# Projecting attention heads with fixed weights, and sending the inverse sums through DRAM: layer 3 of a four-layer graph network

## The chip, the core and the metric

The kernel runs on one core of one Trainium2 chip. The time is the device time of one execution in microseconds (us). The core has a matrix engine (PE) with its weight loads (PEld), a vector engine (DVE), a scalar engine (ACT), a general engine (POOL), and a sync engine (SP) that here issues nearly all DMAs. Each engine works through its own queue in order and waits on semaphores of the others.

## The reference

Sixteen graphs ("batches") of 1024 nodes with 64 features go through four layers over one adjacency matrix, each followed by a residual and a normalisation. The change is in layer 3 only, which computes, per batch:

```python
h = jnp.einsum('bnc,hdc->bhnd', x, Wh)             # 4 heads of 64 channels
out_h = _gat_layer(h, mask, bh)                    # softmax(h h^T, masked) h + bias, per head
cat = jnp.transpose(out_h, (0, 2, 1, 3)).reshape(B, N, H * D)
z = leaky_relu(cat, 0.2)
h2 = jnp.einsum('bnk,dk->bnd', z, Wo)              # 256 channels to 64
out2 = _gat_layer(h2, mask, bo)                    # the outer attention, one head
z2 = leaky_relu(out2, 0.2)                         # then a layer norm with gamma, beta
```

Afterwards the residual with x and one more normalisation give the output of the batch.

## The kernel before

Layer 3 takes a little over two thirds of the time. Its heads are worked in two pairs, n = 0 and n = 1. A pair's attention is 16 **units** (8 blocks of 128 nodes by 2 halves h of 512 nodes). A unit has four steps: `scores` on PE (L1336, two 64-row matmuls into a PSUM tile `s` from a ring of three buffers), an exponential on ACT (L1340, with a constant `shift` per batch and pair that keeps it in range, into a tile `e` from a ring of 11), a mask product on DVE (L1344), and `product` on PE (L1351), which adds the unit to the unnormalised output `y` with channels on partitions and nodes along the row. One value column is all ones, so one channel of each head (rows 63 and 127 of the pair) holds the softmax sum. The outer attention has 8 units of the same kind (L1438, L1443, a sum on DVE at L1448, the mask at L1456, L1463).

The units of a batch are dealt into eight **bursts**, written out by hand: bursts 0 to 3 have five units of the heads, bursts 4 to 7 three of the heads and two outer units of the batch before. `run` puts a burst j into the queues in this order: pending small steps (`catch_up`), the scores and exponentials of the burst, tasks hung on the burst as **mids**, the products of the burst before (`drain`), the masks of this burst, tasks hung on it as **slots**. Engines keep that order.

```python
            catch_up()
            made = [(unit, unit[0]()) for unit in burst]
            tasks(mids, b, j)
            while roots:
                roots.pop(0)()
            drain()
            made = [(product, mask(e)) for (_, mask, product), e in made]
            waiting.extend(lambda product=product, e=e: product(e) for product, e in made)
            ...
            tasks(slots, b, j)
```

From the heads to the outer attention a batch has a **chain** of tasks, each with a place (burst, counted from the start of its batch, so that 8 is burst 0 of the next one):

- `project(q)`, four times (pair by half; 3, 5, 7, 9 mids). The half of `y` was copied to the tile `yT` by ACT (L1357). PE multiplies each 128-node block of it, as the stationary operand, with the weights `wb` (L1366), which gives nodes on partitions and, in two extra columns, the sums. DVE copies the sums (L1370), takes reciprocals (L1372), multiplies (L1376) and applies the leaky relu (L786) into `z`.
- `z_T(n)`, twice (8 mids, 9 slots): eight transposes on PE (L1399) and an ACT copy (L1400) turn a pair's `z` back to channels on partitions, `zT`.
- `h_2T` (10 mids): PE multiplies `zT` with `woT` (L1411), first for n = 0, then n = 1; ACT copies the result to `h2T` (L1415) and squares it; DVE copies two halves across (L1417, L1418).
- `shift_of` (11 mids): PE sums the squares (`pn`, L1273), DVE takes the maximum `top` (L1277), POOL spreads it over partitions (`gtop`, L1279), and the step `below` on ACT turns it into `shift` (L1284). `below` waits in the list `soon`, which `catch_up` puts at the start of the next burst.
- `h_2v` (12 mids): transposes of `h2T`. The first outer units are in burst 12.

After the outer units the ends of a batch follow: `gather` (18 mids: transposes `po2` on PE, L1493, and the product v, L1507, on DVE), `layer` (bias bo and leaky, 18 slots), mean and centre (L726 to L732, 19 slots), and further normalising steps up to the store of `res` by SP. The last two batches and the one before have places of their own. The same functions also prepare the head projections of the next two batches (`prep_x`, `prep_h` with further calls of `shift_of`).

Of the kernel before, what the change touches and what calls it, by code (L numbers as in the profile page):

```python
# [8 lines left out]
F32 = mybir.dt.float32  # L9
# [4 lines left out]
ALU = mybir.AluOpType  # L14
AX = mybir.AxisListType

P = 128
# [565 lines left out]
def fast_path(  # L583
# [24 lines left out]
    nc = tc.nc  # L608
    B, N, D = x.shape
    C = N // P  # L610
    H = L3_Wh.shape[0]
    HD = H * D
    NP = HD // P
    GB = 4
    NG = B // GB
    HALF = N // 2
    CH = C // 2
# [3 lines left out]
    small = ctx.enter_context(tc.tile_pool(name="small", bufs=4))  # L621
# [23 lines left out]
    ident = const.tile([P, P], F32, tag="ident", name="ident")  # L645
# [139 lines left out]
    def leaky(dst, v):  # L785
        nc.vector.scalar_tensor_tensor(dst, v, ALPHA, v, ALU.mult, ALU.max)  # L786
# [407 lines left out]
    woT = const.tile([P, NP, D], F32, tag="woT", name="woT")  # L1194
    wb = const.tile([P, NP, P + 2], F32, tag="wb", name="wb")
    pair_ones = const.tile([P, 2], BF16, tag="pair_ones", name="pair_ones")
    sums = const.tile([P, B, H + 1, C], F32, tag="sums", name="sums")
# [55 lines left out]
    def nodes_adj(c):  # L1253
# [9 lines left out]
            nc.vector.tensor_tensor(own, own, ident16, ALU.max)  # L1263

        return convert
    xT2, hTs, shifts, vals, zs = {}, {}, {}, {}, {}

    def shift_of(key, sq):

# [57 lines left out]
    def heads(b, n):  # L1327
        held = {}

        def scores(k, h):  # L1330
            s = ps_s.tile([P, 2, HALF], F32, tag="s", name="s")
            hT = hTs[b, n][0]
            cols = slice(h * HALF, (h + 1) * HALF)
            for i in range(2):
                rows = slice(i * D, (i + 1) * D)
                nc.tensor.matmul(  # L1336
                    s[:, i, :], hT[rows, k * P : (k + 1) * P], hT[rows, cols], start=True, stop=True
                )
            e = l3.tile([P, 2, HALF], F32, tag="e", name="e", bufs=11)
            nc.scalar.activation(e, s, AF.Exp, bias=shifts[b, n])  # L1340
            return e

        def mask(k, h, e):
            nc.vector.tensor_tensor(e, e, bc_mid(aT[:, k, h * HALF : (h + 1) * HALF], 2), ALU.mult)  # L1344
            return e

        def product(k, h, e):
            if k == 0:
                held[h] = ps_h.tile([P, HALF], F32, tag=f"acc{h * (1 - n)}", name=f"y_{b}_{n}_{h}")
            for i in range(2):  # L1350
                nc.tensor.matmul(  # L1351
                    held[h][i * D : (i + 1) * D, :], vals[b][:, k, :], e[:, i, :],
                    start=(k == 0), stop=(k == C - 1),
                )
            if k == C - 1:
                held["y"] = l3.tile([P, HALF], F32, tag="y", name=f"yT_{b}_{n}_{h}", bufs=1)
                nc.scalar.copy(held["y"], held[h])  # L1357

        def project(q):

            if n == 0 and q == 0:
                zs[b] = l3.tile([P, C, HD], F32, tag="z", name=f"z_{b}", bufs=1)
            pt = ps_s.tile([P, 2, HALF], F32, tag="s", name="po")
            o = pt[:, :, : 2 * (P + 2)].rearrange("p t (c f) -> p t c f", c=2)
            for j in range(CH):
                nc.tensor.matmul(  # L1366
                    o[:, j // 2, j % 2, :], held["y"][:, j * P : (j + 1) * P], wb[:, n, :], start=True, stop=True,
                )
            total = sums[:, b, 2 * n : 2 * n + 2, q * CH : (q + 1) * CH]
            nc.vector.tensor_copy(total.rearrange("p i (t c) -> p t c i", t=2), o[:, :, :, P : P + 2])  # L1370
            rt = small.tile([P, 2, CH], F32, tag="rt3", name="rt3")
            nc.vector.reciprocal(rt, total)  # L1372
            v = l3.tile([P, CH, P], F32, tag="v3", name="v3", bufs=1)
            for i in range(2):
                cols = slice(i * D, (i + 1) * D)
                nc.vector.tensor_tensor(  # L1376
                    v[:, :, cols].rearrange("p (t c) d -> p t c d", t=2), o[:, :, :, cols],
                    rt[:, i].rearrange("p (t c) -> p t c", t=2).unsqueeze(3).to_broadcast([P, 2, 2, D]), ALU.mult,
                )
            leaky(zs[b][:, q * CH : (q + 1) * CH, n * P : (n + 1) * P], v)  # L1380

        units = [
            (lambda k=k, h=h: scores(k, h), lambda e, k=k, h=h: mask(k, h, e), lambda e, k=k, h=h: product(k, h, e))
            for h in range(2) for k in range(C)
        ]
        return units, project


    BURSTS, LAST = 8, 5

    def prep_out(b):
        st = {}

        def z_T(n):
            if n == 0:
                st["zT"] = l3.tile([P, NP, N], F32, tag="zT", name=f"zT_{b}", bufs=1)
            pt = ps_s.tile([P, C, P], F32, tag="s", name="pzT")
            for c in range(C):
                nc.tensor.transpose(pt[:, c, :], zs[b][:, c, n * P : (n + 1) * P], ident)  # L1399
            nc.scalar.copy(st["zT"][:, n, :], pt.rearrange("p c q -> p (c q)"))  # L1400

        def h_2T():


            hT = l3.tile([P, 2, HALF], F32, tag="h2T", name=f"h2T_{b}", bufs=1)
            sq = l3.tile([P, HALF], BF16, tag="h2sq", name=f"h2sq_{b}", bufs=1)
            hTs[b] = hT, sq
            pt = one_bank("ph2T")
            for n in range(NP):
                for h in range(2):  # L1410
                    nc.tensor.matmul(  # L1411
                        pt[h * D : (h + 1) * D, :], woT[:, n], st["zT"][:, n, h * HALF : (h + 1) * HALF],
                        start=(n == 0), stop=(n == NP - 1),
                    )
            nc.scalar.copy(hT[:, 0, :], pt)  # L1415
            nc.scalar.activation(sq, hT[:, 0, :], AF.Square)
            nc.vector.tensor_copy(hT[:D, 1, :], hT[D:, 0, :])  # L1417
            nc.vector.tensor_copy(hT[D:, 1, :], hT[:D, 0, :])  # L1418

        def h_2v():  # L1420
            v = l3.tile([P, C, D], F32, tag="h2v", name=f"h2v_{b}", bufs=1)
            pt = one_bank("ph2v").rearrange("p (c d) -> p c d", c=C)
            for c in range(C):
                nc.tensor.transpose(pt[:, c, :], hTs[b][0][:D, c // CH, c % CH * P : (c % CH + 1) * P], ident[:D, :D])
            nc.scalar.copy(v, pt)
            vals["out", b] = v

        return z_T, h_2T, h_2v
# [245 lines left out]
    with tc.tile_pool(name="ps_g", bufs=1, space=bass.MemoryType.PSUM, reuse_waits="tile") as ps_g, tc.tile_pool(  # L1674
        name="ps_u", bufs=2, space=bass.MemoryType.PSUM, reuse_waits="tile"
# [34 lines left out]
        for q, todo in enumerate(l1_tasks):  # L1710
            t = 7 + 2 * q
            places = (t, 0), (t, 2), (t, 4), (t, 6), (t + 2, 2), (t + 2, 7), (t + 3, 5)
# [13 lines left out]
    with tc.tile_pool(name="l1", bufs=2, reuse_waits="tile") as pool:  # L1726
# [36 lines left out]
        for g in range(NG):  # L1763
# [8 lines left out]
            st = pool.tile([P, C * GB, 6], F32, tag="st1", name=f"st{g}")  # L1772
# [5 lines left out]
            y = xg[g].rearrange("p c b d -> p (c b) d")  # L1778
# [21 lines left out]
    slots, mids = {}, {}  # L1800
    work = [[heads(b, n) for n in range(NP)] for b in range(B)]
    outs = [(prep_out(b), head_out(b)) for b in range(B)]
    E = B - 1
# [7 lines left out]
        at((c + 1) // BURSTS, (c + 1) % BURSTS, lambda convert=convert: convert["go"]())  # L1811
    for b in range(B):
        z_T, h_2T, h_2v = outs[b][0]
        parts = [lambda p=work[b][n][1], q=q: p(q) for n in range(NP) for q in range(2)]
        chain = [
            *parts[:2], lambda z_T=z_T: z_T(0), *parts[2:], lambda z_T=z_T: z_T(1), h_2T,
            lambda b=b: shift_of(b, hTs[b][1]), h_2v,
        ]
        ends = outs[b][1][1]

        places = [(3, mids), (5, mids), (8, mids), (7, mids), (9, mids), (9, slots), (10, mids), (11, mids), (12, mids)]
        places += [(18, mids), *((j, slots) for j in (18, 19, 19, 20, 22, 24, 24, 24, 25, 28))]
        if b == E - 2:
            places[9:] = [(17, mids), *((j, slots) for j in (17, 17, 18, 18, 20, 20, 21, 22, 22, 24))]
        elif b == E - 1:
            places[9:] = [(j, slots) for j in (15, 15, 15, 15, 15, 17, 17, 17, 18, 18)]
        elif b == E:
            places[2] = 7, mids
            places[4:] = [(j, slots) for j in [7] * 5 + [10] * 11]
        for task, (j, where) in zip(chain + ends, places):  # L1830
            t = min(j // BURSTS, E - b)
            at(b + t, j - t * BURSTS, task, where)
# [33 lines left out]
    with tc.tile_pool(name="ps_g", bufs=1, space=bass.MemoryType.PSUM, reuse_waits="tile") as ps_g, tc.tile_pool(  # L1866
        name="ps_p", bufs=1, space=bass.MemoryType.PSUM, reuse_waits="tile"
    ) as ps_p:
        places = [(15, j) for j in (0, 1, 2, 3, 4, 5, 6, 7)]
# [16 lines left out]
    l3 = ctx.enter_context(tc.tile_pool(name="l3", bufs=2, reuse_waits="tile"))  # L1886
    ps_h = ctx.enter_context(tc.tile_pool(name="ps_h", bufs=1, space=bass.MemoryType.PSUM, reuse_waits="tile"))
    ps_s = ctx.enter_context(tc.tile_pool(name="ps_s", bufs=3, space=bass.MemoryType.PSUM, reuse_waits="tile"))
    rings["s"] = ps_s
    aN = l3.tile([P, C, N], BF16, tag="aN", name="aN", bufs=1)  # L1890

    def tasks(where, b, j):
        for task in where.get((b, j), []):
# [110 lines left out]
```

## Time and profile before

| What | Before |
|---|---|
| Median of 3 runs | 2073.36 us (2067.45 to 2074.19) |
| Span of the profiled execution | 2072.9 us |
| PE busy | 1963.8 us |
| DVE busy | 1795.8 us |
| ACT busy | 1293.9 us |
| POOL busy | 70.1 us |
| Granted PE clock, mean | 0.982 |

The profiled execution's own time is its span of 2072.9 us, 0.5 us below the median of the runs. A row of the costliest groups gives line, engine, operation, output and inputs with shapes, count, then busy us and mean ns, then the idle time before it and what ended it. A row of the timeline gives start and length in us, then the same names, with the idle time of that engine before it in brackets. A row of busy times gives a stretch, its length, then the busy us of PE, PEld, DVE, ACT and POOL (with instruction counts), the granted clock, and the DMA share and rate. A row of DMA issues gives count, size of one, and the median us to landing. PE, f32 matmuls show as two instructions each. Line numbers are those of the kernel before unless said otherwise; the changed file is longer by up to 35 lines from this place on.

### The profile page before, as it was taken

What the parts mean: (1) busy time and instruction counts of PE and PEld (TensorE: products, weight loads), DVE (VectorE), ACT (ScalarE), POOL (GpSimd) and SP (SyncE); (2) the same over time, 40 slices, a digit from 0 to 9 for tenths busy, and PEclk for the clock granted to TensorE, in tenths of its full rate; (3) what the DMA queues carried; (4) which work ended last, traced back from release to release, by engine and by line L of the source; (5) the groups of instructions that cost most, each with busy time, mean ns of one, the idle gap of its engine ahead of it and who ended that gap; (6) DMA issues with size and microseconds to landing.
All of it is one profiled execution on the core that took longest, in us unless ns stands there. A gap on an engine that the chain in (4) does not pass through costs nothing.

```text
span 2072.9 us, 26628 instructions
## 1 busy us (share of the span) xinstructions
PE 1963.8 (95%) x10041; PEld 854.1 (41%) x10041; DVE 1795.8 (87%) x3147; ACT 1293.9 (62%) x2250; POOL 70.1 (3%) x77
## 2 busy tenths in 40 slices
PE   7999989998898999999999999999999999999985
PEld 4444347753332343343343434434343343433432
DVE  5899988879998777889898898988989889889996
ACT  4466568676778666666666656656665665665543
POOL 0000000000000000000000000000000000000001
PEclk9999999999999999999999999999999999999997
DMA  7000000000000200000000000000000000000000
GB/s 170 1 1 1 1 1 1 1 1 1 1 1 11 71 1 1 1 1 6 1 6 6 1 6 6 1 6 1 6 1 6 6 1 6 6 1 6 1 6 17
DMA packets 23657, 18.92 MB, mean 9 GB/s; under 512 B 19361, under 2 KB 19426, under 8 KB 23522
## 3 DMA queue, kind: packets, MB, share of 16 engines
q1 hardware_dynamic: 23218, 17.11, 3.0%
q8 instruction: 81, 1.33, 0.3%
q14 instruction: 54, 0.44, 0.1%
q10 hardware_dynamic: 304, 0.03, 0.0%
HBM read 12.95 MB, written 4.19 MB: 8 GB/s over the span
## 4 chain that ended last, share of the span: by engine, by line
PE 47%; DVE 37%; ACT 11%; issue 3%; DMA 0%; POOL 0%; SPq 0%; DVEq 0%; POOLq 0%; ACTq 0%
DVE e L1344 13%; PE y L1351 10%; PE s L1336 8%; DVE e L991 6%; PE y_l L1003 6%; ACT e L1340 6%; PE po L1735 5%; DVE e L1456 4%; DVE junk L1448 4%; PE u_l L1015 3%; PE y L1463 2%; PE po L1366 2%; ACT e L1443 2%; PE s L1438 2%; DVE v L1376 2%
## 5 line engine op out<-in xcount | busy, mean ns | idle before, releaser
L1340 ACT ACTIVATE e<-s,shift 128x1024 f32<-128x1024 f32 x512 | 542.8, 1119 | 335.3 <-PE s L1336 334.3
L1344 DVE TENSOR_TENSOR e<-e,aT 128x1024 f32<-128x1024 f32 x512 | 600.7, 1217 | 4.9 <-ACT e L1340 4.8
L1351 PE MATMUL y<-e,vals 128*64 128x512 f32 x2048 | 489.5, 600 | 11.0 <-DVE e L1344 5.9
L1336 PE MATMUL s<-hT 64*128 64x512 f32 x2048 | 497.8, 605 | 1.3 <-ACT e L1340 0.9
L991 DVE SCALAR_TENSOR_TENSOR e<-G_l,q,aT 128x1024 f32<-128x1024 f32 x256 | 315.3, 1274 | 4.4 <-ACT G_l L968 4.4
L1336 PEld LDWEIGHTS s<-hT 64*128 64x128 f32 x2048 | 186.9, 187 | 279.7 <-issue 141.1
L1003 PE MATMUL y_l<-e,vals_l 128*64 128x512 f32 x1024 | 257.7, 624 | 25.4 <-DVE e L991 18.7
L1351 PEld LDWEIGHTS y<-e,vals 128*64 128x64 f32 x2048 | 134.9, 136 | 277.8 <-issue 189.6
L1456 DVE TENSOR_TENSOR e<-e,aT 128x1024 f32<-128x1024 f32 x128 | 156.3, 1224 | 8.3 <-ACT e L1443 1.9
L1448 DVE SCALAR_TENSOR_TENSOR junk<-e,aN 128x1024 bf16<-128x1024 f32 x120 | 146.1, 1218 | 0.0
L1443 ACT ACTIVATE e<-s,shift 128x1024 f32<-128x1024 f32 x128 | 142.0, 1115 | 1.3 <-PE s L1438 1.1
L1463 PE MATMUL y<-e,h2v 128*64 128x512 f32 x512 | 131.2, 595 | 1.5 <-DVE e L1456 1.5
L1438 PE MATMUL s<-h2T 64*128 64x512 f32 x512 | 131.7, 596 | 0.0
L1003 PEld LDWEIGHTS y_l<-e,vals_l 128*64 128x64 f32 x1024 | 63.6, 140 | 160.8 <-issue 78.4
L1735 PE MATMUL po<-hi,aR 128*128 128x512 f32 x256 | 104.1, 407 | 11.1 <-ACT hi L1664 7.3
L1735 PE MATMUL po<-lo,aR 128*128 128x512 f32 x256 | 102.3, 400 | 0.0
L1279 POOL PARTITION_ALL_REDUCE gtop<-top x48 | 42.7, 890 | 1375.9 <-DVE top L1277 1236.4
L780 ACT ACTIVATE x<-m,bn_shift,bn_rstd 128x64 f32<-128x64 f32 x256 | 88.5, 431 | 0.5 <-DVE bn_shift L771 0.5
L1366 PE MATMUL po<-wb,yT 128*128 128x130 f32 x512 | 74.2, 288 | 10.1 <-ACT e L1340 9.4
L1366 PEld LDWEIGHTS po<-wb,yT 128*128 128x128 f32 x512 | 61.9, 190 | 47.4 <-ACT e L1340 45.8
L1438 PEld LDWEIGHTS s<-h2T 64*128 64x128 f32 x512 | 49.8, 188 | 61.2 <-issue 29.5
L1400 ACT COPY zT<-pzT 128x1024 f32<-128x1024 f32 x32 | 32.8, 1025 | 66.9 <-PE pzT L1399 66.9
(246 smaller groups left out, 2028.5 us busy)
## 6 DMA issues: line engine op xcount, KB each, us to landing
adj<-in_adj_dram SPq DMA_DIRECT2D x16, 512.0 KB, 3.9
x<-in_x_dram SPq DMA_DIRECT2D x16, 256.0 KB, 5.3
out_dram<-res SPq DMA_DIRECT2D x16, 256.0 KB, 2.0
wl<-in_L_gnn_Wh_dram SPq DMA_DIRECT2D x2, 64.0 KB, 3.2
wo<-in_L_gnn_Wo_dram SPq DMA_DIRECT2D x1, 64.0 KB, 2.8
l_wd<-in_L_gnn_W_dram ACTq DMA_DIRECT2D x2, 16.0 KB, 4.6
l_wd<-in_L_gnn_W_dram SPq DMA_DIRECT2D x2, 16.0 KB, 2.0
bo<-in_L_gnn_bo_dram SPq DMA_DIRECT2D x1, 32.0 KB, 3.0
```

Of the source, the lines that this page charges most:

```text
L991: nc.vector.scalar_tensor_tensor(e, G[b - b % 2][:, b % 2, :], pq[b - b % 2][1][:, k, b % 2 : b % 2 + 1], aT[:, k, :], ALU.max, ALU.mult,)
L1003: nc.tensor.matmul(held["y"][h * D : (h + 1) * D, :], vals[b][:, k, :], e[:, h * HALF : (h + 1) * HALF], start=(k == 0), stop=(k == C - 1),)
L1336: nc.tensor.matmul(s[:, i, :], hT[rows, k * P : (k + 1) * P], hT[rows, cols], start=True, stop=True)
L1340: nc.scalar.activation(e, s, AF.Exp, bias=shifts[b, n])
L1344: nc.vector.tensor_tensor(e, e, bc_mid(aT[:, k, h * HALF : (h + 1) * HALF], 2), ALU.mult)
L1351: nc.tensor.matmul(held[h][i * D : (i + 1) * D, :], vals[b][:, k, :], e[:, i, :], start=(k == 0), stop=(k == C - 1),)
L1366: nc.tensor.matmul(o[:, j // 2, j % 2, :], held["y"][:, j * P : (j + 1) * P], wb[:, n, :], start=True, stop=True,)
L1438: nc.tensor.matmul(s[:, i, :], hT[rows, (i + k // CH) % 2, k % CH * P : (k % CH + 1) * P], hT[rows, 0, :], start=True, stop=True,)
L1443: nc.scalar.activation(e, s, AF.Exp, bias=shifts[b])
L1448: nc.vector.scalar_tensor_tensor(junk.rearrange("p c q -> p (c q)").bitcast(BF16), e.rearrange("p i q -> p (i q)"), 1.0, aN[:, k, :], ALU. ...
L1456: nc.vector.tensor_tensor(e, e, aT[:, k, :].rearrange("p (i q) -> p i q", i=2), ALU.mult)
L1735: nc.tensor.matmul(po.rearrange("p q k f -> p (q k f)"), aR[:, k, ic * P : (ic + 1) * P], e[:, k].rearrange("p q k f -> p (q k f)"), start ...
```

## The change

For all pairs but the last of the last batch, the four `project` parts and two `z_T` of a batch become three tasks per pair. `project_T` keeps `wb` as the stationary operand and streams `yT` (now both halves in one tile), so the result stays with channels on partitions and is copied to `zT` by ACT. The sums go another way: SP writes the two sum rows of `yT` to DRAM and reads them back into `sums`, laid over partitions; `inverse` takes the reciprocals there, writes them to a second DRAM row, and SP reads that row back broadcast over 64 partitions for each head, into the tile `r`. `quotient` multiplies `zT` with `r` and applies the leaky relu. The last pair of batch 15 keeps `project` and `z_T`. The places in the chain change too.

```diff
             if k == C - 1:
-                held["y"] = l3.tile([P, HALF], F32, tag="y", name=f"yT_{b}_{n}_{h}", bufs=1)
-                nc.scalar.copy(held["y"], held[h])
+                if h == 0:
+                    held["y"] = l3.tile([P, 2, HALF], F32, tag="y", name=f"yT_{b}_{n}", bufs=1)
+                nc.scalar.copy(held["y"][:, h, :], held[h])
+                if h and not late:
+                    rows = dram.tile([2, N], F32, tag="rows", name=f"rows_{b}_{n}")
+                    for i in range(2):
+                        nc.sync.dma_start(
+                            rows[i : i + 1, :],
+                            held["y"][(i + 1) * D - 1 : (i + 1) * D].rearrange("p h q -> p (h q)"),
+                        )
+                    nc.sync.dma_start(
+                        sums[:, b, 2 * n : 2 * n + 2, :], rows.rearrange("i (p j) -> p i j", j=C)
+                    )
+
+        def project_T():
+
+            if n == 0:
+                zTs[b] = l3.tile([P, NP, N], F32, tag="zT", name=f"zT_{b}", bufs=1)
+            pt = ps_s.tile([P, 2, HALF], F32, tag="s", name="poT")
+            for h in range(2):
+                nc.tensor.matmul(pt[:, h, :], wb[:, n, :P], held["y"][:, h, :], start=True, stop=True)
+            nc.scalar.copy(zTs[b][:, n, :], pt.rearrange("p h q -> p (h q)"))
+
+        def inverse():
+            rt = small.tile([P, 2, C], F32, tag="rt3", name="rt3")
+            nc.vector.reciprocal(rt, sums[:, b, 2 * n : 2 * n + 2, :])
+            rows = dram.tile([2, N], F32, tag="inverse", name=f"inverse_{b}_{n}")
+            nc.sync.dma_start(rows.rearrange("i (p j) -> p i j", j=C), rt)
+            held["r"] = l3.tile([P, N], F32, tag="r", name=f"r_{b}_{n}", bufs=1)
+            for i in range(2):
+                nc.sync.dma_start(held["r"][i * D : (i + 1) * D, :], rows[i].partition_broadcast(D))
+
+        def quotient():
+            z = zTs[b][:, n, :]
+            nc.vector.tensor_tensor(z, z, held["r"], ALU.mult)
+            leaky(z, z)
...
+        late = b == B - 1 and n == NP - 1
...
-        return units, project
+        if late:
+            return units, [lambda: project(0), lambda: project(1)]
+        return units, [project_T, inverse, quotient]
...
-        parts = [lambda p=work[b][n][1], q=q: p(q) for n in range(NP) for q in range(2)]
         chain = [
-            *parts[:2], lambda z_T=z_T: z_T(0), *parts[2:], lambda z_T=z_T: z_T(1), h_2T,
+            *work[b][0][1], *work[b][1][1], *([z_T] if b == E else []), h_2T,
             lambda b=b: shift_of(b, hTs[b][1]), h_2v,
         ]
...
-        places = [(3, mids), (5, mids), (8, mids), (7, mids), (9, mids), (9, slots), (10, mids), (11, mids), (12, mids)]
+        places = [(5, mids), (5, slots), (7, mids), (9, mids), (9, slots), (10, slots), (11, mids), (11, slots), (12, mids)]
...
         elif b == E:
-            places[2] = 7, mids
+            places[3] = 7, mids
```

More of the change, by code (lines that the diff above doesn't have):

```diff
@@ L1265, in nodes_adj @@
         return convert
-    xT2, hTs, shifts, vals, zs = {}, {}, {}, {}, {}
+    xT2, hTs, shifts, vals, zs, zTs = {}, {}, {}, {}, {}, {}
     def shift_of(key, sq):
@@ L1355, in product @@
             if k == C - 1:
-                held["y"] = l3.tile([P, HALF], F32, tag="y", name=f"yT_{b}_{n}_{h}", bufs=1)
-                nc.scalar.copy(held["y"], held[h])
+                if h == 0:
[30 more added lines that the diff above has]
+            leaky(z, z)
         def project(q):
-            if n == 0 and q == 0:
-                zs[b] = l3.tile([P, C, HD], F32, tag="z", name=f"z_{b}", bufs=1)
+            if q == 0:
+                zs[b] = l3.tile([P, C, P], F32, tag="e", name=f"z_{b}", bufs=11)
             pt = ps_s.tile([P, 2, HALF], F32, tag="s", name="po")
@@ L1366, in project @@
                 nc.tensor.matmul(
-                    o[:, j // 2, j % 2, :], held["y"][:, j * P : (j + 1) * P], wb[:, n, :], start=True, stop=True,
+                    o[:, j // 2, j % 2, :], held["y"][:, q, j * P : (j + 1) * P], wb[:, n, :], start=True, stop=True,
                 )
@@ L1379, in project @@
                 )
-            leaky(zs[b][:, q * CH : (q + 1) * CH, n * P : (n + 1) * P], v)
+            leaky(zs[b][:, q * CH : (q + 1) * CH, :], v)
+        late = b == B - 1 and n == NP - 1
         units = [
@@ L1385, in heads, with z_T @@
         ]
-        return units, project
+        if late:
+            return units, [lambda: project(0), lambda: project(1)]
+        return units, [project_T, inverse, quotient]
     BURSTS, LAST = 8, 5
     def prep_out(b):
[L1392 to L1396, printed above, removed]
+        def z_T():
             pt = ps_s.tile([P, C, P], F32, tag="s", name="pzT")
             for c in range(C):
-                nc.tensor.transpose(pt[:, c, :], zs[b][:, c, n * P : (n + 1) * P], ident)
-            nc.scalar.copy(st["zT"][:, n, :], pt.rearrange("p c q -> p (c q)"))
+                nc.tensor.transpose(pt[:, c, :], zs[b][:, c, :], ident)
+            nc.scalar.copy(zTs[b][:, NP - 1, :], pt.rearrange("p c q -> p (c q)"))
         def h_2T():
@@ L1411, in h_2T @@
                     nc.tensor.matmul(
-                        pt[h * D : (h + 1) * D, :], woT[:, n], st["zT"][:, n, h * HALF : (h + 1) * HALF],
+                        pt[h * D : (h + 1) * D, :], woT[:, n], zTs[b][:, n, h * HALF : (h + 1) * HALF],
                         start=(n == 0), stop=(n == NP - 1),
@@ L1890, in fast_path @@
     aN = l3.tile([P, C, N], BF16, tag="aN", name="aN", bufs=1)
+    dram = ctx.enter_context(tc.tile_pool(name="dram", bufs=2, space=bass.MemoryType.DRAM))
     def tasks(where, b, j):
```

## The prediction

> **What bounds the kernel now.** I read the page first, then the busy times over two batches of layer 3, the timeline of bursts 2 to 4 of batch 10, and the DMA issues.
>
> ```profile
> PE 1963.8 (95%) x10041; PEld 854.1 (41%) x10041; DVE 1795.8 (87%) x3147; ACT 1293.9 (62%) x2250; POOL 70.1 (3%) x77
> ...
> L1366 PE MATMUL po<-wb,yT 128*128 128x130 f32 x512 | 74.2, 288 | 10.1 <-ACT e L1340 9.4
> ```
>
> ```profile
> 1503.90:1675.50 171.60, 168.84 (x844) 68.51 (x840) 152.19 (x223) 107.72 (x135) 5.40 (x6) 1.00 0.01 4
> ```
>
> In two batches of 85.8 us each, PE (second number) is busy 168.84 of 171.60 us, DVE (fourth) 152.19, ACT (fifth) 107.72, at a granted clock of 1.00. PE is the bound and has no holes, so what is taken from PE is gained, unless a wait comes in its place. Whether one does is read from the order of the queues:
>
> ```profile
> 1516.39 4.56 PE L1336 MATMUL s<-hT 64*128 64x512 f32 x20
> ...
> 1521.57 0.69 DVE L1507 TENSOR_TENSOR v<-po,rt 128x512 f32<-128x512 f32 x1 [2.89 <-PE po L1493]
> 1521.74 1.94 PE L1411 MATMUL ph2T<-zT,woT 128*64 128x512 f32 x8 [0.21 <-ACT e L1340]
> ...
> 1524.35 0.42 DVE L1417 COPY h2T<-h2T 64x512 f32<-64x512 f32 x1 [2.08 <-ACT h2T L1415]
> ...
> 1525.33 5.75 DVE L1344 TENSOR_TENSOR e<-e,aT 128x1024 f32<-128x1024 f32 x5
> ...
> 1528.34 4.56 PE L1336 MATMUL s<-hT 64*128 64x512 f32 x20
> ...
> 1533.53 0.35 POOL L1279 PARTITION_ALL_REDUCE gtop<-top  x1 [6.78 <-DVE top L1277]
> 1533.70 1.16 PE L1366 MATMUL po<-wb,yT 128*128 128x130 f32 x8 [0.61 <-ACT e L1340]
> ...
> 1536.73 5.76 DVE L1344 TENSOR_TENSOR e<-e,aT 128x1024 f32<-128x1024 f32 x5
> ...
> 1539.23 1.13 PE L1336 MATMUL s<-hT 64*128 64x512 f32 x4
> ...
> 1540.40 1.11 ACT L1340 ACTIVATE e<-s,shift 128x1024 f32<-128x1024 f32 x1 [5.58 <-PE s L1336]
> ...
> 1542.41 0.68 DVE L726 TENSOR_REDUCE ln_sum<-v 128x8 f32<-128x512 f32 x1
> ...
> 1544.05 0.69 DVE L732 TENSOR_TENSOR m<-v 128x512 f32<-128x512 f32 x1
> ```
>
> Bursts 2, 3 and 4 begin on PE at 1516.39, 1528.34 and 1539.23. DVE runs the masks of burst 3 only from 1536.73 and ends that burst's list at 1544.74, 5.5 us after PE began burst 4. Nobody minds, because ACT's exponentials of burst 4 (1540.40) wait for PE alone. The shift that they need was reduced at 1533.53, in the middle of burst 3, ahead of those masks.
>
> **Removed.** One `po` part holds PE for 1.09 us (start to next start, 1508.77 to 1509.86), a `pzT` group 1.02 us (1515.37 to 1516.38). A batch has four and two: 4.36 + 2.04 = 6.4 us. On DVE a part is 1.84 us (1509.97 to 1511.81: copy, reciprocal, two products, leaky), four 7.4. At burst 3 PE also waited 0.6 us between `pn` and `po` for a PSUM buffer; that goes.
>
> **Added.** Two `project_T`, each two f32 matmuls 128*128 by 512 columns. Nearest row: L1336's unit of 64-row pairs, two instructions of 512 columns each way, starts every 0.86 us (1539.76 to 1540.62), so two take 1.72, with 0.1 for the change of operation 1.8. Upper end from the 130-column rows: 1.09/8 x 512/130 = 0.54 per instruction, 2.15 for four; those rows include weight loads, so I take 1.8, or 3.6 a batch. ACT copies two `zT` as before. DVE gets a reciprocal (0.2) and a product and a leaky of 128x1024 (1.2 each, as L1344) per pair: 5.2 instead of 7.4 us a batch. PE's net over all bursts, with the ring wait and the smaller gaps in bursts 7 and 0, is -3.5 us a batch.
>
> **The DMA legs.** Per pair SP issues two rows out, one 32-byte-piece read into `sums`, one such write, two broadcasts of 256 KB.
>
> ```profile
> x<-in_x_dram SPq DMA_DIRECT2D x16, 256.0 KB, 5.3
> out_dram<-res SPq DMA_DIRECT2D x16, 256.0 KB, 2.0
> ...
> wa<-in_L_gnn_wa_dram SPq DMA_DIRECT2D x2, 0.2 KB, 3.4
> ```
>
> A leg lies between the 2.0 of the big store and the 5.3 of the crowded load; 4-byte pieces took 3.4. First trip (rows, then sums): 4 to 8 us. It starts with the ACT copy at the end of burst 4 or 8 and is wanted by `inverse` after the masks of burst 5 or 9, 12 us later: hidden. Second trip (write, then broadcasts): 4 to 8.7 us. For n = 1 the reciprocal stands last in DVE's list of burst 9, which I expect to end up to 3 us into burst 10; `quotient` has its turn 12.8 us into burst 10. So 9.8 us or more is there: hidden, with 1 us to spare at the worst end. For n = 0 the cover is the masks of burst 6 (8.35 us, 1565.52 to 1573.87) with their small ends, about 10 us. If the cover fails, each us of lateness moves everything below by a us. SP's `res` stores queue behind waits for rows, but nothing needs their buffers soon.
>
> [...]
>
> **Moved: the shift.** `h_2T` goes from burst 10 to 11 (mids), `shift_of` from 11 mids to 11 slots; the first outer units are still in burst 12. In the changed program's order, DVE's queue from burst 10 (call it 2 of the next batch) reads: v of `gather`, masks(2), bo and leaky, quotient and its leaky, ln_step, h2T copies, masks(3), mean and centre of the batch before, and only then `top`. ACT's queue puts `below`, which waits for POOL and so for `top`, ahead of all exponentials of burst 4, the inner ones too. What is queued behind it: five exponentials, hence PE's fourth score (three PSUM buffers, one held by `pn`), hence everything.
>
> I place it from burst 2's first score (0), even batch:
> - v starts at 5.2 (1521.57 - 1516.39), masks(2) at 6.1 instead of 8.9, since the h2T wait left; 5.7 later bo; bo 0.7, leaky 0.6; quotient from 13.1 to 15.6.
> - PE: scores, po2 and pn, products: 4.5 + 0.9 + 0.3 + 4.4, so burst 3 starts at 10.1. Scores to 14.6, first half of ph2T to 15.4, second half waits 0.2 for the quotient, to 16.6.
> - ACT copies h2T to 17.3; DVE's two copies to 18.2; masks(3) to 23.9; mean and centre 2.3; `top` at 26.1.
> - PE: products(2) to 21.0, pn, burst 4 from 21.3. Undisturbed its first exponential is at 22.5 (+1.17 as in 1539.23 to 1540.40).
> - From `top` to a usable shift: POOL starts 0.34 after `top` (1533.19 to 1533.53), runs 0.35, `below` 0.3: 1.07 in all. So the first exponential is at 27.2: **4.7 us late**, and PE stands for as long. For other shifts L1279 runs 1.17 instead of 0.35; then 5.5.
>
> Odd batches have no pn in burst 2 and a `pxT` (1.0) in burst 3 of PE: the exponential at 26.9 instead of 23.2, **3.7 late**. DVE, at 87% before and relieved by 2, follows in the later bursts: its masks of burst 7 end about 1 us before PE's products want them.
>
> **The sum.** Even: -3.5 + 0.2 + 4.7 = +1.4; odd: -3.3 + 0.2 + 3.7 = +0.6. Batches 2 to 14: 7 x 1.4 + 6 x 0.6 = 13.4. Batch 0 gains 1.5; in batch 1 no ends lie in DVE's list, so the wait is 1.4 and it gains 1.7; batch 15, whose list has other ends, loses 3. The tail, where PE waits for DVE in the last burst (5.90 us at 2011.50), gets a quotient of 2.4 and loses a part: +1.5. Together +14.7. The profiled span is 2072.9 us, 0.5 below the median of the runs, 2073.36: **2088**.
>
> **Rivals.**
> 1. Faster: the wait is covered. Point: `top` must start by about 0.1 us after burst 4's first score; I have 4.8 and 3.8. The break-even is 1.4 us earlier than mine (even). For it: if DVE started masks(2) without waiting for po2, 5 us would be found. Against it: `gather` stands ahead of them in the queue. Price: all of -3.2 x 15 = -48, so 2025; half the wait gone gives 2060.
> 2. The second DMA trip outlasts its cover by 2 to 3 us (32-byte writes, broadcasts of one row 64 times). The quotient, and all below it, is later by as much: 2088 + 14 x 2.5 = 2123.
> 3. Gain and wait cancel within what a measurement here can tell from no change (0.3%, 6 us): my errors of 0.8 us a batch (POOL's 1.17, PE's 2.15, starts of DVE) make 12 us in sum. 2073.
> 4. The projection is not shorter on PE: at 2.15 each, 0.7 a batch more, 2098; this lies in my own range.
>
> **How the numbers follow.** Forecast with its errors (about 2074 to 2103): 0.55. Rival 1: 0.15. Rival 2: 0.12. Rival 3: 0.18. The range leaves out the full gain and the late end of rival 2: 2060 to 2115. Faster by over 0.3% is rival 1 and 0.02 of rival 3: 0.17. The same is the rest of rival 3 and 0.04 from the low edge of the forecast: 0.2. Slower is the rest of the forecast and rival 2: 0.63.
>
> **What would show it.** In the changed trace: PE holes of some 4 us at burst 4 of every batch, put down to ACT or the ring; ACT's `shift` (L1284) waiting for POOL `gtop` in 15 places with 3 to 5 us; `po` and `pzT` gone but for the last batch, `poT` at 1.8; DVE quotient (L1390) without idle time before it. Wrong if burst 4's exponentials start 1.2 us after its scores, or if L1390 waits for DMA.

## The result, and the profile after

The changed kernel takes 2084.95 us in the median of 4 runs (2082.08 to 2088.34), beside 2070.4 us (2066.51 to 2074.19) for the kernel before: a ratio of 1.0076, with a 95% interval of 1.0054 to 1.0099. It is 14.6 us slower. Its profiled execution has a span of 2086.1 us (before 2072.9) at a mean granted clock of 0.973 (before 0.982).

From the page of the changed kernel, the busy times and two of its groups:

```profile
PE 1948.1 (93%) x9421; PEld 790.8 (38%) x9421; DVE 1763.0 (85%) x2930; ACT 1296.6 (62%) x2250; POOL 69.3 (3%) x77
...
L1336 PE MATMUL s<-hT 64*128 64x512 f32 x2048 | 510.4, 618 | 40.0 <-DVE top L1277 37.1
...
L1284 ACT ACTIVATE shift<-gtop,headroom 128x1 f32<-128x1 f32 x48 | 14.4, 300 | 141.9 <-POOL gtop L1279 141.7
```

Work went away as planned: PE has 620 instructions fewer, and DVE is busy 32.8 us less. PE is busy only 15.7 us less, where experiment 6 below, with the same 9421 instructions, has 48.1 less: part of PE's work runs here at half the clock, as is seen further down. The rest of the time came back as a wait. PE stood 37.1 us ahead of scores, and the releaser named is `top`. ACT stood 141.7 us ahead of `shift`; not all of that is new, since ACT idles at the start of burst 4 anyway. Where it happens is seen in the timeline of the changed kernel, from burst 2 to burst 4 of an even batch, the place that the prediction walked through (start, length, operation, idle time before it):

```profile
1521.48 4.56 PE L1336 MATMUL s<-hT 64*128 64x512 f32 x20
...
1522.81 0.38 SPq L1383 DMA_DIRECT2D inverse<-rt  x1
...
1524.44 1.09 SPq L1386 DMA_DIRECT2D r<-inverse  x2
...
1534.38 1.22 DVE L1390 TENSOR_TENSOR zT<-zT,r 128x1024 f32<-128x1024 f32 x1
...
1539.55 5.77 DVE L1344 TENSOR_TENSOR e<-e,aT 128x1024 f32<-128x1024 f32 x5
...
1542.40 1.13 PE L1336 MATMUL s<-hT 64*128 64x512 f32 x4
...
1547.48 0.16 DVE L1277 TENSOR_REDUCE top<-pn 128x1 f32<-128x8 f32 x1
1547.70 2.08 PE L1336 MATMUL s<-hT 64*128 64x512 f32 x4 [3.31 <-DVE top L1277]
1547.81 0.35 POOL L1279 PARTITION_ALL_REDUCE gtop<-top  x1 [19.00 <-DVE top L1277]
1548.20 0.29 ACT L1284 ACTIVATE shift<-gtop,headroom 128x1 f32<-128x1 f32 x1 [8.91 <-POOL gtop L1279]
1548.40 1.10 ACT L1340 ACTIVATE e<-s,shift 128x1024 f32<-128x1024 f32 x1
```

PE begins burst 4 at 1542.40, and before the change its first exponential followed 1.17 us later. Now it comes at 1548.40, 6.00 us later, so it is 4.83 us late. In the 5 us before that, DVE was running the masks of burst 3 and the mean and centre, and `top` came behind them. PE computes two scores ahead, fills its ring and stands. Both waits end with `top`: ACT's for the shift, and PE's for the buffer that `pn` holds until `top` has read it. No run tells what either would cost alone.

The stand has a second face, a slower clock, seen in the busy times of the changed kernel over burst 4 (stretch, its length, then PE, PEld, DVE, ACT, POOL, the granted clock, DMA share and rate):

```profile
1542.00:1544.00 2.00, 2.00 (x14) 0.85 (x12) 2.00 (x2) 0.00 (x0) 0.00 (x0) 1.00 0.00 0
1544.00:1546.00 2.00, 0.39 (x2) 0.00 (x0) 1.97 (x4) 0.00 (x0) 0.00 (x0) 1.00 0.00 0
...
1549.00:1550.00 1.00, 1.00 (x4) 0.46 (x4) 0.00 (x0) 1.00 (x2) 0.00 (x0) 0.50 0.05 16
...
1551.00:1552.00 1.00, 1.00 (x7) 0.35 (x4) 0.00 (x0) 1.00 (x2) 0.00 (x0) 1.00 0.00 0
```

The granted clock is 0.50 when PE starts again and back at 1.00 at 1551. The first scores after the stand take 2.08 us in place of 1.13. In this batch that adds nothing to the lateness: the next scores, at 1549.57, had to wait in any case until ACT's first exponential (1548.40 to 1549.50) gave back a buffer. Burst 4's first and last exponential of the heads are 3.99 us apart (1548.40 to 1552.39), as before the change (1540.40 to 1544.40): ACT's five exponentials, one after the other, set that pace. Burst 5 then starts 14.88 us after burst 4 (1542.40 to 1557.28), where it was 10.06 (1539.23 to 1549.29): 4.82 more, the lateness and no more. It is not so everywhere. In batch 2 the clock stayed at 0.50 for 6.83 us (from 847.65), and although the first exponential was as late as here (6.00 us after the first scores), burst 5 started 16.43 us after burst 4 (842.83 to 859.26), 1.55 more than in this batch.

### The profile page after: what moved, and what is told of

It is laid out like the page before. It is cut to its first block, busy times and chain, and to the rows that moved or that the text cites. A ratio compares the mean times of both kernels' runs of the same rounds, so it can differ in the third digit from the quotient of the medians.

```text
span 2086.1 us, 25442 instructions
## 1 busy us (share of the span) xinstructions
PE 1948.1 (93%) x9421; PEld 790.8 (38%) x9421; DVE 1763.0 (85%) x2930; ACT 1296.6 (62%) x2250; POOL 69.3 (3%) x77
## 4 chain that ended last, share of the span: by engine, by line
PE 65%; DVE 23%; ACT 9%; issue 2%; SPq 0%; DMA 0%; POOL 0%; POOLq 0%; DVEq 0%; ACTq 0%
PE s L1336 17%; PE y L1351 16%; DVE e L1344 7%; DVE e L991 6%; PE y_l L1003 6%; PE po L1770 5%; PE y L1498 4%; PE s L1473 4%; ACT e L1340 3%; PE u_l L1015 3%; PE poT L1376 3%; PE phT L1310 1%; PE ph2T L1446 1%; ACT x L780 1%; ACT e L1478 1%
## 5 line engine op out<-in xcount | busy, mean ns | idle before, releaser
L1336 PE MATMUL s<-hT 64*128 64x512 f32 x2048 | 510.4, 618 | 40.0 <-DVE top L1277 37.1
L1003 PE MATMUL y_l<-e,vals_l 128*64 128x512 f32 x1024 | 256.3, 621 | 26.9 <-DVE e L991 20.1
L1473 PE MATMUL s<-h2T 64*128 64x512 f32 x512 | 145.0, 650 | 2.9 <-ACT e L1340 2.8
L1284 ACT ACTIVATE shift<-gtop,headroom 128x1 f32<-128x1 f32 x48 | 14.4, 300 | 141.9 <-POOL gtop L1279 141.7
L1277 DVE TENSOR_REDUCE top<-pn 128x1 f32<-128x16 f32 (+1 forms) x48 | 8.1, 168 | 83.8 <-PE pn L1273 83.8
L1498 PEld LDWEIGHTS y<-e,h2v 128*64 128x64 f32 x512 | 36.6, 138 | 76.2 <-issue 57.4
```

Of the source, the lines that this page charges most:

```text
L1003: nc.tensor.matmul(held["y"][h * D : (h + 1) * D, :], vals[b][:, k, :], e[:, h * HALF : (h + 1) * HALF], start=(k == 0), stop=(k == C - 1),)
L1336: nc.tensor.matmul(s[:, i, :], hT[rows, k * P : (k + 1) * P], hT[rows, cols], start=True, stop=True)
L1473: nc.tensor.matmul(s[:, i, :], hT[rows, (i + k // CH) % 2, k % CH * P : (k % CH + 1) * P], hT[rows, 0, :], start=True, stop=True,)
L1498: nc.tensor.matmul(held["o"][h * D : (h + 1) * D, :], vals["out", b][:, k, :], e[:, h, :], start=(k == 0), stop=(k == C - 1),)
```

## The experiments

The theory: the projection itself gains about 3 us a batch on PE, and the new place of the shift (`top` behind the masks of burst 3 and the ends of the batch before, `below` ahead of all exponentials of burst 4) costs 4.8 us in even and 3.7 us in odd batches. The rivals: the DMA trips are late, or the projection is no gain on PE. The first four kernels ran on one chip beside the kernel before at 2069.58 us, the other four on another beside 2067.12 us; each ratio is to the kernel before on its own chip. All edits but that of the fifth are to the changed kernel.

**1. Only the shift's place put back** ahead of the masks, from the end of burst 11 to its middle.

```diff
-places = [..., (9, mids), (9, slots), (10, slots), (11, mids), (11, slots), (12, mids)]
+places = [..., (9, mids), (9, slots), (10, slots), (11, mids), (11, mids), (12, mids)]
```

> The changed kernel with one place altered: the outer shift (shift_of) is taken in the middle of burst 11, not at its end. Theory A (the new cost is ACT's wait for the shift, 4.8 us in even and 3.7 us in odd batches, because `top` stands last in DVE's list): the maximum is then taken ahead of the masks of burst 3, ACT no longer waits at burst 4; PE instead waits some 1.4 us in burst 3 for the squares of h2T. About 40 us less than the changed kernel, near 2045. Theory B (the DMA legs, or the projection on PE, eat the gain): no change, near 2085.

Measured: 2043.28 us (2038.67 to 2047.41), ratio 0.9874 (0.9848 to 0.9901). One word takes the kernel from 0.8% slower to 1.3% faster. Its timeline at the same place of a batch:

```profile
1510.10 0.17 DVE L1277 TENSOR_REDUCE top<-pn 128x1 f32<-128x8 f32 x1 [0.19 <-PE pn L1273]
...
1514.37 1.13 PE L1336 MATMUL s<-hT 64*128 64x512 f32 x4
1515.54 1.11 ACT L1340 ACTIVATE e<-s,shift 128x1024 f32<-128x1024 f32 x1 [3.61 <-PE s L1336]
```

`top` now lies 4.3 us ahead of burst 4's scores, and the exponential again comes 1.17 us after them, released by PE. Another wait takes part of the gain, in the list of PE's waits (line, releaser, us in total, times, longest):

```profile
PE pn L1273 <- ACT h2sq L1451: 21.6, 16, 1.4
```

With `h_2T` and the shift in the same place, PE's sum `pn` follows `h_2T` at once and waits for ACT's square.

**2. `h_2T` and the shift earlier, with `quotient` earlier too.**

```diff
-places = [..., (9, mids), (9, slots), (10, slots), (11, mids), (11, slots), (12, mids)]
+places = [..., (9, mids), (9, slots), (10, mids), (10, slots), (11, mids), (12, mids)]
```

> The changed kernel with three places moved: the quotient of the second pair in the middle of burst 10 (not its end), h_2T at the end of burst 10, shift_of in the middle of burst 11. Theory A: all of the new wait goes and nothing replaces it, so 2085 - (7 x 4.8 + 6 x 3.7 + some 6 for batches 1 and 15) = about 2023, if the broadcast inverse is there by 6 us into burst 10. Theory B (DMA legs late): the quotient, now 7 us earlier, waits for DMA several us and the time stays at 2085 or rises.

Measured: 2033.8 us (2032.24 to 2039.47), ratio 0.9833 (0.9811 to 0.9855). It is faster than the first, but 11 us short of what I expected. The timeline shows where the second DMA trip runs out of cover (the write, the two broadcasts, the product):

```profile
1484.12 0.38 SPq L1383 DMA_DIRECT2D inverse<-rt  x1
...
1485.74 1.09 SPq L1386 DMA_DIRECT2D r<-inverse  x2
...
1490.23 1.23 DVE L1390 TENSOR_TENSOR zT<-zT,r 128x1024 f32<-128x1024 f32 x1 [1.26 <-DMA r<-inverse]
```

The reciprocals end at 1484.09 and `r` is there at 1490.23, so the second trip takes 6.1 us: 1.6 to the broadcasts' issue and 4.5 for these. With `quotient` in the middle of burst 10 this is not hidden; 14 quotients waited 37.9 us in all. My expectation had made it a condition that `r` is there 6 us into burst 10; here it came 7.0 us into it (burst 10 starts at 1483.10).

**3. Both broadcasts of `r` sent twice**, to see how near the trip is to its cover in the changed kernel.

```diff
                 nc.sync.dma_start(held["r"][i * D : (i + 1) * D, :], rows[i].partition_broadcast(D))
+                nc.sync.dma_start(held["r"][i * D : (i + 1) * D, :], rows[i].partition_broadcast(D))
```

> The changed kernel with each broadcast of the inverse row issued twice (124 transfers of 256 KB in place of 62; the quotient waits for the last). Theory A: the transfers lie beside other work with several us to spare, so 0 to 3 us more. Theory B (the second trip through DRAM sets when the quotient runs): 2 us or more a batch, 30 us or more in all.

Measured: 2090.79 us (2088.49 to 2095.63), ratio 1.01 (1.0076 to 1.0124). The interval overlaps that of the changed kernel, 1.0054 to 1.0099, so the times alone do not tell the two apart. The rows do. Of the idle time of engines around the tile `r`, by what ended it (us, times), the third kernel's profile gives the following, all of it ahead of the product; the changed kernel has no such row:

```profile
  DMA r<-inverse: 15.7, 9
```

So the trip is hidden in the changed kernel, and with twice its broadcasts it is not hidden everywhere. The rival of late DMAs is out. The doubled trips behind these nine waits took 9.6 to 11.6 us from the issue of the write to `r`; the single ones that were waited for in experiment 2 took 6.0 to 6.6. The cover that they are to fit into, from the end of the reciprocals to `quotient`, is 10.0 us or more in 29 of the changed kernel's 31 places, and 7.2 and 8.0 in the other two (the first pair of batch 0, the second of batch 14).

**4. The ends moved away**: mean and centre of the batch before, from the end of burst 19 (burst 3 of the next batch but one) to that of burst 20, and the shift left where the change put it.

```diff
-places += [(18, mids), *((j, slots) for j in (18, 19, 19, 20, 22, 24, 24, 24, 25, 28))]
+places += [(18, mids), *((j, slots) for j in (18, 20, 20, 20, 22, 24, 24, 24, 25, 28))]
```

> The changed kernel with mean and centre of the batch before moved from the end of burst 19 to the end of burst 20, so that they no longer stand ahead of `top` in DVE's list. Theory A: `top` is 2.3 us earlier, the wait of 4.8 or 3.7 us shrinks by that in batches 2 to 14: 13 x 2.3 = 30 us less, near 2055. Theory B: DVE's total work is the same, so no change.

Measured: 2060.85 us (2053.47 to 2064.54), ratio 0.9947 (0.9926 to 0.9968), 1.3% below the changed kernel. PE's wait:

```profile
PE s L1336 <- DVE top L1277: 8.4, 8, 1.1
```

The 37.1 us of PE's stand went to 8.4, and no stand is over 1.1 us. So what counts is whatever lies ahead of `top` in DVE's list: with mean and centre out of its way, some 27 us come back (1.0076 less 0.9947, of 2070). The first exponential of burst 4 is now 2.56 us late in even batches and 1.38 in odd ones, 2.27 less in each; the masks are still ahead of `top`.

**5. The shift's place alone, in the kernel before.**

```diff
-places = [..., (10, mids), (11, mids), (12, mids)]
+places = [..., (10, mids), (11, slots), (12, mids)]
```

> The kernel before with one place altered: shift_of at the end of burst 11 instead of its middle, nothing else of the change. Theory A: `top` then follows masks, mean and centre, 5.5 us (even) or 4.6 us (odd) after burst 4 begins on PE, so the first exponential is 5.4 or 4.6 us late; 7 x 5.4 + 6 x 4.6 + 5 for batches 1 and 15 = 70, less 0.6 a batch for a PSUM wait in burst 3 that goes: about 60 more than before, near 2130. Theory B (the wait needs the quotient and its DMA legs): no change, 2070.

Measured: 2131.73 us (2129.93 to 2134.91), ratio 1.0308 (1.0279 to 1.0338). With the old projection and no DMA trip the same move costs 64.6 us, 4.3 for each of 15 batches. PE waits for the same `top` as in the changed kernel:

```profile
PE s L1336 <- DVE top L1277: 42.9, 15, 3.5
```

The cost belongs to the place, not to the projection.

**6. All of it**: as in the second, and `inverse` one step earlier, so that the second trip has its cover back.

```diff
-places = [..., (9, mids), (9, slots), (10, slots), (11, mids), (11, slots), (12, mids)]
+places = [..., (9, mids), (9, mids), (10, mids), (10, slots), (11, mids), (12, mids)]
```

> As the early version (quotient in the middle of burst 10, h_2T at its end, shift_of in the middle of burst 11) with the inverse of the second pair moved to the middle of burst 9, one set of masks sooner. The early version showed DVE waiting 37.9 us in 14 places for the broadcast row. Theory A: the reciprocal is 6 us earlier, the second trip of 6.1 us is over before the quotient, and some 10 us go: near 2022. Theory B (those waits were covered for PE): no change, 2034.

Measured: 2023.28 us (2021.01 to 2029.85), ratio 0.9791 (0.9759 to 0.9823), faster than both kernels. From its page:

```profile
PE 1915.7 (95%) x9421; PEld 784.6 (39%) x9421; DVE 1761.6 (87%) x2930; ACT 1295.1 (64%) x2250; POOL 82.1 (4%) x77
```

A quotient waited for `r` once, 0.6 us. PE's waits for the shift's `top` are gone from its list, and of those for `h2sq` one of 1.3 us is left. Between the second kernel and this one lies only the place of `inverse`, and the two ratios are 0.4% apart, though their intervals overlap by a little, so the step from one to the other is shown by the waits more than by the time.

**7 and 8. One product of DVE more, ahead of the shift or elsewhere.** Both add a product of 128x1024 per batch whose result nobody uses; in 7 it stands directly ahead of the shift, in 8 at the end of burst 0.

```diff
+        def extra():
+            junk = l3.tile([P, CH, P], F32, tag="v3", name="junk", bufs=1)
+            nc.vector.tensor_tensor(
+                junk.rearrange("p c q -> p (c q)").bitcast(BF16), zTs[b][:, n, :], held["r"], ALU.mult
+            )
...
+        if b < E:
+            shift, extra = chain[7], work[b][1][2]
+            chain[7] = lambda shift=shift, extra=extra: (extra(), shift())   # 7
+            at(b + 1, 0, work[b][0][2])                                      # 8, in place of the two lines above
```

> The changed kernel with one more product of 128x1024 on DVE (its result is not used) in each of batches 1 to 15, right ahead of `top` in DVE's list. Theory A: `top` and so everything is 1.2 us later, 15 x 1.2 = 18 us more, near 2103. Theory B (DVE is not what sets the wait): within 3 us of 2085.

> The changed kernel with the same additional product at the end of burst 0 of batches 1 to 15, where DVE's list ends some us before the po2 of burst 2 that it has to wait for. Theory A: hidden, 0 to 3 us more, near 2086. Theory B (DVE's total work is the bound): 18 us more, near 2103.

Measured: 7 takes 2104.37 us (2103.05 to 2111.28), ratio 1.0183 (1.015 to 1.0216); 8 takes 2086.81 us (2084.62 to 2089.04), ratio 1.0093 (1.0064 to 1.0122), not to be told from the changed kernel. PE's waits in 7:

```profile
PE s L1336 <- DVE top L1277: 53.9, 15, 4.4
```

The longest stand went from 3.31 to 4.44 us, and 7 lies 17.6 us over 8: 1.17 a batch, where two products in DVE's queue start 1.13 us apart. The first exponential of burst 4 is 1.13 us later than in the changed kernel in 7 (7.13 us after the first scores at 1551.39, where it was 6.00), and at the same place as there in 8. So the path runs through DVE's queue to `top`, at full price, and the same work at the end of burst 0 is free.

## Why the prediction was right

The prediction held in its time, its sign and its mechanism. Step by step:

- **The chain to the shift.** Counted from burst 2's first score, even batch, predicted and measured: quotient 13.1 and 12.9, `top` 26.1 and 26.0, burst 4's start 21.3 and 20.9, first exponential 27.2 and 26.9. Lateness 4.7 and 4.83 in even batches, 3.7 and 3.65 in odd ones (scores at 1628.41, exponential at 1633.23). The walk through the queues in order was the whole of the prediction, and it was good to 0.4 us.
- **"PE stands for as long".** Only in effect. PE stands 3.31 us (odd: 2.14), since its ring lets it run two scores ahead, and then goes at the pace of ACT's exponentials, in part at half clock. The prediction did not have the half clock.
- **The projection's gain.** Taken at -6.4 us for two batches. The sixth kernel, which has the projection without the stand, repeats every 165.8 us against 171.65 before: -5.9. The term that was off is `project_T`: taken at 1.8 us, it holds PE for 1.92 (1561.77 to 1563.69). Four of them make 0.48 us in two batches, nearly all of the difference. My upper end of 2.15 and the fourth rival were too high. On DVE 2.2 us a batch were to go; 32.8 us less in all is 2.1 for each of 15.5.
- **The sum.** It came out closer than its terms. Two batches were to cost +2.0; once settled they cost +2.45 (174.1 against 171.65). Batches 2 to 14 took 19.2 us more, from the first score of batch 2 to that of batch 15, where I had 13.4. Of these 5.8 us, 2.9 are the 0.45 for each two batches; most of the rest lies in the first of them (batch 2 grew by 2.87, batch 3 by 1.90, the settled ones by 1.3 and 1.15), where the half clock took time of its own, a term that I did not have. Batches 0 and 1 gained 1.0 and 1.5 (I had 1.5 and 1.7). Batch 15 lost 2.5 from its first burst to its last (3), but the tail behind that was 2.0 shorter, where I had a loss of 1.5. Layer 3 and what follows it are thus 17.3 us longer in the profile, and the part ahead of layer 3, which the change does not touch, was 4.1 us shorter in that execution (652.4 against 656.5; the ten profiles go from 650.1 to 656.5). By the medians the whole is +14.6 where the sum was +14.7. That it fits this closely is luck: terms that were too small and too large by 3 to 6 us offset one another. The two large terms for two batches, the gain and the lateness, are each within about 0.5 us.
- **The DMA trips.** Hidden, as predicted. The second takes 6.1 us where experiment 2 shows it bare, inside the 4 to 8.7 taken. The cover that I had, 9.8 us or more for the second pair and about 10 for the first, held in 29 of 31 places; the two at 7.2 and 8.0 us still covered a trip of some 6.5, though not my worst end of 8.7. The write in 32-byte pieces was the smaller part of the second trip: 1.6 us from its issue to that of the broadcasts which wait for it (2.7 and 3.5 in two of the 31), beside the 2.0 from issue to landing of the large stores before the change. The two broadcasts took the larger part, 4.5.
- **Rival 1, faster.** Its point was `top` 4.8 us earlier. Experiment 1 moved it there, and experiment 6 came to 44 us below before, where the rival was priced at 48. It lost to the place alone. **Rival 3** (gain and wait cancel) lost by the 0.8%.
- **What I said the trace would show.** The holes at burst 4 are there, released by DVE's `top` rather than by ACT. The count for `shift` is 24 waits and 141.7 us, where I had 15 with 3 to 5 each. That row counts all of ACT's idle time before the shift (8.91 in an even batch), of which ACT would have had a part anyway; the first exponential's distance from burst 4's first score reads the loss rightly.

## What to carry to other kernels

A step that moves down an in-order queue takes with it everyone who waits for it (64.6 us for one such move, in experiment 5): before a task is put "at the end" of a stage, list what then stands ahead of it on its own engine, and what is queued behind the wait on the other. Here 620 saved matmul instructions lost against one word in a list of places, and with four places mended the same change gains 2%. The DMA round trip was free here only where its cover was longer than its measured time (no wait in the changed kernel, 37.9 us of waits in experiment 2), so time the trip where it stands bare (6.1 us here) before moving its consumer forward.

## What the runs showed of the hardware that I had not expected

**The granted clock fell to 0.50 with stands of PE, and a stand's length alone does not tell whether it falls.** In the changed kernel the granted clock was 0.50 for 3.41 us (once 6.83) at or soon after each of its 14 stands at burst 4, seven of 3.31 us, six of 2.14 and one of 1.06. But in the fifth kernel the stands of 2.60 us, in six odd batches, left it at 1.00; and in the fourth, where PE stands 1.06 us and soon after 0.72 us for ACT, it fell in three of eight batches, 2.1 to 2.4 us after the first of these stands. A stand of the fifth kernel with the 3.41 us behind it, and the fall in the fourth:

```profile
1661.60:1664.21 2.61, 0.01 (x2) 0.00 (x0) 2.46 (x6) 0.00 (x0) 0.00 (x0) 1.00 0.00 0
1664.21:1667.62 3.41, 2.69 (x12) 0.91 (x12) 1.58 (x2) 2.91 (x4) 0.35 (x1) 1.00 0.00 0
...
1530.18:1533.59 3.41, 3.41 (x16) 1.73 (x12) 0.00 (x0) 3.08 (x4) 0.00 (x0) 0.50 0.00 0
```

In that batch of the fourth kernel burst 5 started 13.64 us after burst 4, and 12.61 in one without a fall: 1.03 us, with the exponentials equally late. The stretches of half clock in layer 3 of the changed kernel start whole multiples of 3.413 us apart (847.65, 936.40, 1025.14 and 1110.48 us: 26, 26 and 25 of them). So where a stand falls against such a grid may decide; no run here was made to test it.

**POOL's reduction takes 0.35 or 1.17 us**, always of a 128x1 input. In the timeline of the first kernel, DVE and POOL at one such moment:

```profile
1520.26 1.22 DVE L1344 TENSOR_TENSOR e<-e,aT 128x1024 f32<-128x1024 f32 x1
...
1520.51 1.17 POOL L1279 PARTITION_ALL_REDUCE gtop<-top  x1 [8.91 <-DVE top L1277]
```

The mask, a product of two SBUF tiles, runs until 1521.48, and POOL ends 0.20 us later. In the changed kernel at 1547.81, with DVE idle, the reduction takes 0.35. Of the 48 reductions on this line in the changed kernel's trace, 30 are long, and each of them began 0.25 us after the start of a DVE operation with two input tiles, 1.2 us long. One took 0.64 us, beside a product of 0.68. Of the 17 short ones, 14 found DVE idle, one began 0.04 us ahead of a mask, one met a sum with a single input (L736), and one met the last 0.11 us of an 8-column product. What holds POOL up in the long rows they do not show, and no run here was made to test it. A wait of DVE is not seen: the mask that POOL was ahead of took 1.23 us, where the mean of all masks of the heads is 1.22. It matters for the shift: placed in the middle of masks, as in experiments 1, 2 and 6, it pays 0.8 us more for POOL, and has time for it there.
